# Summing a group's gathered tiles in the opposite order, and two Ifs in a row for two paths

## The chip, the cores and the metric

The kernel runs on one core of one Trainium2 chip. The metric is the device time of one execution in microseconds (us), the median of several executions; lower is better. The profile comes from one further execution under the hardware profiler, which has a time of its own.

## The reference

One layer of a graph network on N = 12500 nodes with D = 256 features and E = 200000 edges, all in float32. The edges come sorted by destination `dst`.

```python
h = relu(layernorm(x))                       # 12500 x 256
agg = segment_sum(h[src], dst, N)            # 200000 gathered rows, summed by destination
z = (1 + eps_gin) * h + agg
t = relu(batchnorm(z @ W1 + b1, g1, bt1))    # 256 -> 512, statistics over all nodes
y = relu(batchnorm(t @ W2 + b2 + h, g2, bt2))
out = x + y
```

## The kernel before

**Two paths.** The kernel first loads `src` and `dst`, transposes them on TensorE so that each column holds the 128 edges of one tile, and tests whether the destinations are spread evenly enough. A flag of 0 or 1 comes out (L205), each engine loads it into a register (L689) and branches on it (L690). `fast()` (L263) handles even spreads, which is the case for these inputs; `general()` (L474) handles the rest and is not executed.

**Stages of `fast()`.** Nodes are handled in 25 chunks of 512 (the last has 212).

1. Layer norm: each chunk of `x` is loaded, normalized to `ht`, stored to the table `h_tab` in HBM, and transposed into `hT`, which stays in SBUF.
2. Gather stage. The 1563 edge tiles of 128 edges (the last has 64) form 131 groups of 12 (`GT`), the last of 3. `gather(i)` (L322 to L333) issues one indirect DMA per tile from POOL (L328); each fetches 128 rows of 1 KB from `h_tab` into a slice of the group's buffer `gt`. The loop over the tiles at L326 runs backwards, and the list `gs` keeps the tiles in that order of issue. There are three such buffers (`AHEAD + 1`), so the gathers of group i can start only when the sums of group i - 3 have read theirs.
3. `sums(i)` (L349 to L372): VectorE makes the one-hot matrices `oh` of the group (L353); then one float32 matmul per tile adds its rows into the 128 x 256 PSUM tile `ps` (L361 to L365), in the order of `gs`. The trace records each float32 matmul as two weight loads and two matmuls, so a group has 24 records of L362. ScalarE copies `ps` to `zs` (L367), and VectorE makes the placing matrix `at` (L369).
4. `put(i)` (L374 to L389): two matmuls (four records, L380) spread the group's sums over a window of 280 nodes in `pz`, and VectorE adds the window to the chunks' `zc` (L389).
5. `first_layer(c)` (L391 to L404): once a chunk is complete, eight matmuls (16 records, L397) make `t = z @ W1`; VectorE takes statistics (L401), ScalarE copies (L402), and SP stores to `t_tab` in HBM (L403).
6. Second layer (L428 to L446) after the first batch norm's statistics are complete, and the output stage (L454 to L472) after the second's.

**What sets the order of the work.** The loop at L409 to L420 writes it out: the gathers of group i + 2, the sums of group i, the placing of group i - 1, then any chunk that is complete. A tile scheduler merges it into one queue per engine, each of which runs in order. In the queue of TensorE the first one or two tiles of a group's sums can stand ahead of a chunk's `first_layer`. POOL's queue holds, in this stage, only gathers.

**Semaphores.** A DMA adds to one of eight semaphores of the gathers in turn, so the semaphore of a gather is also that of the gather eight earlier, and POOL waits for that one before it reuses it. In the built program each matmul of L362 waits for the semaphore of its own tile's gather and then adds 1 to TensorE's own count. The two branches issue different numbers of DMAs; so that all counts agree where the branches meet, the program of before adds the difference at the start of the fast branch, for the gathers by eight instructions on POOL, one ahead of each of the first eight gathers.

Of the kernel before, what the change touches and what calls it, by code (L numbers as in the profile page):

```python
# [28 lines left out]
def kernel(  # L29
# [27 lines left out]
    for g in range(NCH):  # L57
        rows = min(CH, N - g * CH)
# [204 lines left out]
    def fast():  # L263
        with ExitStack() as fs:
# [32 lines left out]
            with ExitStack() as es:  # L297
# [51 lines left out]
                def sums(i):  # L349

                    t0, n = groups[i]
                    oh = sel.tile([P, GT, P], F32, name="oh")
                    nc.vector.tensor_tensor(  # L353
                        oh[:, :n, :],
                        col[:, :P].unsqueeze(1).to_broadcast([P, n, P]),
                        dstT[:, t0 : t0 + n].unsqueeze(2).to_broadcast([P, n, P]),
                        op=OP.is_equal,
                    )
                    ga, gs = gathered.pop(i)
                    ps = ps_s.tile([P, D], F32, name="ps")  # L360
                    for k, (j, rows) in enumerate(gs):  # L361
                        nc.tensor.matmul(  # L362
                            ps, lhsT=oh[:rows, j, :], rhs=ga[:rows, j, :], start=(k == 0),
                            stop=(k == n - 1),
                        )  # L365
                    zs = sel.tile([P, D], F32, name="zs", bufs=3)
                    nc.scalar.copy(zs, ps)  # L367
                    at = sel.tile([P, WIDE], F32, name="at")
                    nc.vector.tensor_scalar(  # L369
                        at, col, shift[:, i : i + 1], None, op0=OP.is_equal  # L370
                    )
                    summed[i] = zs, at  # L372
# [36 lines left out]
                for i in range(NG + 1):  # L409
                    if i + AHEAD < NG:  # L410
                        gather(i + AHEAD)
                    if i < NG:
                        sums(i)
                    if i == 0:
                        continue
                    put(i - 1)
                    nxt = span(i)[0] if i < NG else N
                    while done < NCH and min((done + 1) * CH, N) <= nxt:
                        first_layer(done)
                        done += 1  # L420
# [266 lines left out]
                    move(nc.scalar, ot, out, g, store=True)  # L687

    off = nc.values_load(flag, min_val=0, max_val=1, skip_runtime_bounds_check_because="it is 0 or 1")  # L689
    with tc.If(off == 0) as cmp:  # L690
        fast()
    with cmp.Else():
        general()


# [28 lines left out]
```

## Time and profile before

| | us |
|---|---|
| median of 3 runs (2385.66 to 2388.86) | 2385.85 |
| the profiled execution, its own time | 2652.91 |
| its span, first to last instruction | 2651.0 |
| first gather starts | 149.12 |
| last gather starts | 2361.34 |
| first matmul of the second layer starts | 2392.04 |

| engine | busy us | share of the span |
|---|---|---|
| PE (matmul) | 1623.6 | 61% |
| POOL | 1483.4 | 56% |
| PEld (weight load) | 1029.4 | 39% |
| DVE | 633.8 | 24% |
| ACT | 346.8 | 13% |

The gather stage, from 149 to about 2363 us, is over four fifths of the span. How to read the views: a group of instructions has its busy time and the mean of one in ns, then the idle time of its engine just before it and what ended most of that. "issue" means that nothing which the profile shows ended the wait; "remote", in the chain "another core or an unknown queue", that the releaser could not be told. PEclk and the clock column of the stretches are the granted TensorE clock as a share of full speed. [...] A row of the timeline has start us, duration us, engine, line, operation, out<-in, count, and in brackets the idle time before it with its releaser. The ends of matmuls are modelled; their starts are recorded.

### The profile page before, as it was taken

The page shows a single profiled execution, that of the slowest core. Times are in us where ns is not written, and L with a number is a line of the kernel's source. Part 1 is how long each engine was busy: PE and PEld are TensorE (multiplying, and loading weights), DVE is VectorE, ACT ScalarE, POOL GpSimd, SP SyncE. Part 2 cuts the span into 40 slices and gives each one's busy share as a digit, 9 for nine tenths or more (in the row PEclk, how much of TensorE's full clock was granted, in tenths as well). Part 3 has the DMA queues.
Part 4 walks back from the last instruction along what each step waited for, and adds up shares of the span by engine and source line. Part 5 has one row for each costly group of instructions (what it writes and reads, how often), then busy time and mean ns, then how long its engine had stood idle before and what let it go on. Part 6 is the DMA issues. An engine that isn't in the chain of part 4 may idle for free.

```text
span 2651.0 us, 14241 instructions
## 1 busy us (share of the span) xinstructions
PE 1623.6 (61%) x4881; PEld 1029.4 (39%) x4881; DVE 633.8 (24%) x1017; ACT 346.8 (13%) x561; POOL 1483.4 (56%) x1575
## 2 busy tenths in 40 slices
PE   3564556755665576556456556666565656569985
PEld 2333344433443343334334334434343334444444
DVE  6611121211221122112112112121121212124443
ACT  4710000000000000000000000000000000004446
POOL 0056667666766666666676676666666676640000
PEclk6566677776776786767777766767776677779985
DMA  5633333333333333333333333333333333325437
GB/s 176 227 101 90 95 101 115 105 95 101 115 105 95 111 105 105 96 111 105 107 97 109 106 98 102 110 105 112 95 105 110 91 114 102 111 78 214 159 130 281
DMA packets 101342, 310.96 MB, mean 117 GB/s; under 512 B 27684, under 2 KB 32362, under 8 KB 95118
## 3 DMA queue, kind: packets, MB, share of 16 engines
q0 software_dynamic: 75008, 204.90, 26.3%
q1 hardware_dynamic: 21744, 91.21, 9.6%
q10 hardware_dynamic: 4510, 13.86, 1.3%
q8 instruction: 41, 0.67, 0.1%
q14 instruction: 39, 0.32, 0.0%
HBM read 258.66 MB, written 51.20 MB: 117 GB/s over the span
## 4 chain that ended last, share of the span: by engine, by line
issue 28%; PE 26%; POOL 25%; another core or an unknown queue 9%; DMA 3%; DVE 2%; ACT 2%; ACTq 0%; POOLq 0%
POOL gt L328 25%; PE ps L362 13%; PE py L441 6%; PE ph L397 4%; DMA gt<-h_tab,srcT 3%; PE pz L380 2%; ACT yr L460 2%; DVE oh L353 1%; PE po L467 1%; DVE zc L389 1%; DVE ot L471 0%; DVE mv L229 0%; DVE at L369 0%; DVE st L401 0%
## 5 line engine op out<-in xcount | busy, mean ns | idle before, releaser
L328 POOL DMA_INDIRECT gt<-h_tab,srcT x1563 | 1481.8, 948 | 850.5 <-issue 458.2
L362 PE MATMUL ps<-gt,oh 128*128 128x256 f32 x3126 | 987.1, 447 | 643.0 <-issue 559.4
L362 PEld LDWEIGHTS ps<-gt,oh 128*128 128x128 f32 x3126 | 672.5, 221 | 949.5 <-issue 738.8
L389 DVE TENSOR_TENSOR zc<-pz,zc 128x560 f32<-128x560 f32 (+9 forms) x203 | 101.0, 527 | 1518.0 <-PE ps L362 863.5
L380 PE MATMUL pz<-at,zs 128*128 128x280 f32 x524 | 194.5, 498 | 181.4 <-DVE zc L389 114.8
L367 ACT COPY zs<-ps 128x256 f32<-128x256 f32 x131 | 48.9, 373 | 1739.4 <-PE ps L362 1147.3
L397 PE MATMUL ph<-zc,w1s 128*128 128x512 f32 (+1 forms) x400 | 197.0, 648 | 80.4 <-DVE zc L389 56.9
L353 DVE TENSOR_TENSOR oh<-col,dstT 128x1536 f32<-128x1536 f32 x131 | 227.8, 1739 | 14.5 <-issue 14.5
L380 PEld LDWEIGHTS pz<-at,zs 128*128 128x128 f32 x524 | 119.5, 237 | 235.0 <-issue 209.2
L441 PE MATMUL py<-tT,w2s 128*128 128x512 f32 (+1 forms) x400 | 169.5, 587 | 4.6 <-ACT tT L434 4.6
L397 PEld LDWEIGHTS ph<-zc,w1s 128*128 128x128 f32 x400 | 82.4, 211 | 181.1 <-issue 117.5
L401 DVE BATCH_NORM_STATS2 st<-ph 128x6 f32<-128x512 f32 (+1 forms) x100 | 68.4, 684 | 265.9 <-remote 93.7
L441 PEld LDWEIGHTS py<-tT,w2s 128*128 128x128 f32 x400 | 76.4, 192 | 97.7 <-issue 86.7
L402 ACT COPY ts<-ph 128x512 f32<-128x512 f32 (+1 forms) x100 | 57.3, 573 | 334.0 <-DVE st L401 251.9
L285 PE MATMUL pz<-ident,ht 128*128 128x128 f32 (+1 forms) x200 | 65.0, 442 | 54.1 <-ACT ht L259 19.5
L434 ACT ACTIVATE tT<-ti,of,sc 128x512 f32<-128x512 f32 (+1 forms) x100 | 72.3, 796 | 91.3 <-issue 86.4
L467 PE MATMUL po<-ident,yr 128*128 128x128 f32 (+1 forms) x200 | 47.6, 413 | 35.6 <-ACT yr L460 35.6
L285 PEld LDWEIGHTS pz<-ident,ht 128*128 128x128 f32 (+1 forms) x200 | 36.6, 205 | 82.5 <-ACT ht L259 40.7
L369 DVE TENSOR_SCALAR at<-col,shift 128x280 f32<-128x280 f32 x131 | 65.5, 500 | 0.0
L460 ACT ACTIVATE yr<-hT,of,sc 128x512 f32<-128x512 f32 (+1 forms) x50 | 59.9, 1276 | 20.1 <-DVE ot L471 19.2
L445 DVE TENSOR_TENSOR hT<-py,hT 128x512 f32<-128x512 f32 (+1 forms) x50 | 33.9, 678 | 100.9 <-PE py L441 100.9
L467 PEld LDWEIGHTS po<-ident,yr 128*128 128x128 f32 (+1 forms) x200 | 37.5, 214 | 45.7 <-ACT yr L460 45.7
(68 smaller groups left out, 307.6 us busy)
## 6 DMA issues: line engine op xcount, KB each, us to landing
gt<-h_tab,srcT POOLq DMA_INDIRECT x1563
t_tab<-ts SPq DMA_DIRECT2D x24, 1024.0 KB
ti<-t_tab SPq DMA_DIRECT2D x24, 1024.0 KB
xt<-in_x_dram SPq DMA_DIRECT2D x24, 512.0 KB
h_tab<-ht SPq DMA_DIRECT2D x24, 512.0 KB
xr<-in_x_dram SPq DMA_DIRECT2D x24, 512.0 KB
out_dram<-ot ACTq DMA_DIRECT2D x24, 512.0 KB
rawi_d<-in_dst_dram SPq DMA_DIRECT2D x1, 768.0 KB
```

The costliest lines, as they stand in the source:

```text
L285: nc.tensor.transpose(pz[:, d, c * w : (c + 1) * w], ht[:w, c, d * P : (d + 1) * P], ident[:w, :w],)
L328: nc.gpsimd.indirect_dma_start(out=ga[:rows, t - t0, :], out_offset=None, in_=h_tab, in_offset=bass.IndirectOffsetOnAxis(ap=srcT[:rows, t ...
L353: nc.vector.tensor_tensor(oh[:, :n, :], col[:, :P].unsqueeze(1).to_broadcast([P, n, P]), dstT[:, t0 : t0 + n].unsqueeze(2).to_broadcast([P ...
L362: nc.tensor.matmul(ps, lhsT=oh[:rows, j, :], rhs=ga[:rows, j, :], start=(k == 0), stop=(k == n - 1),)
L380: nc.tensor.matmul(pz[:, d, :WIDE], lhsT=zs[:, d * P : (d + 1) * P], rhs=at, start=True, stop=True)
L389: nc.vector.tensor_add(side, pz[:, :, a - lo : b - lo], side)
L397: nc.tensor.matmul(ph[:, :n], lhsT=w1s[:, d, f * P : (f + 1) * P], rhs=zc[c][:, d, :n], start=(d == 0), stop=(d == DC - 1),)
L401: nc.vector.bn_stats(st1[:, f, c, :], ph[:, :n])
L434: nc.scalar.activation(tT[:, f, :n], ti[:, f, :n], AF.Relu, bias=of1[:, f : f + 1], scale=sc1[:, f : f + 1],)
L441: nc.tensor.matmul(py[:, :n], lhsT=w2s[:, f, d * P : (d + 1) * P], rhs=tT[:, f, :n], start=(f == 0), stop=(f == HC - 1),)
L460: nc.scalar.activation(yr[:, d, :, :w], hT[g][:, d, :].rearrange("p (w c) -> p c w", c=R), AF.Relu, bias=of2[:, d : d + 1], scale=sc2[:, d ...
L467: nc.tensor.transpose(po[:w, c, d * P : (d + 1) * P], yr[:, d, c, :w], ident)
```

## The change

There are two edits. The matmuls of a group go through the list of gathers from its end: the first matmul of a group uses the tile that was gathered last. Loop order and instruction count are otherwise the same, and so is the order of the lines in TensorE's queue. The path is chosen by two Ifs, one after the other, each without an Else.

```diff
@@ def sums(i)
                     ga, gs = gathered.pop(i)
                     ps = ps_s.tile([P, D], F32, name="ps")
-                    for k, (j, rows) in enumerate(gs):
+                    for k, (j, rows) in enumerate(reversed(gs)):
                         nc.tensor.matmul(
                             ps, lhsT=oh[:rows, j, :], rhs=ga[:rows, j, :], start=(k == 0),
                             stop=(k == n - 1),
@@ end of tile_gnn_kernel
     off = nc.values_load(flag, min_val=0, max_val=1, skip_runtime_bounds_check_because="it is 0 or 1")
-    with tc.If(off == 0) as cmp:
+    with tc.If(off == 0):
         fast()
-    with cmp.Else():
+    with tc.If(off == 1):
         general()
```

In the program that is built from it, the order of a group's waits changes as follows: in a full group the first matmul waits for the gather that was issued last; the next seven wait for semaphores of earlier gathers, the last four carry no wait, and only the last matmul of the group adds to TensorE's count. The eight semaphore-adding instructions ahead of the first gathers are gone from POOL. At the end of the fast path every engine branches to the second If, compares, and jumps over the general path into a short block that makes up its counts: one addition each on POOL, ACT, PE and DVE, eight on SP, and one instruction on POOL for the gathers' semaphores; then the program ends as before.

## Prediction

> **What bounds the kernel now.** I read the chain of waits first, then the group of gathers, then who makes POOL wait.
>
> ```profile
> issue 28%; PE 26%; POOL 25%; another core or an unknown queue 9%; DMA 3%; DVE 2%; ACT 2%; ACTq 0%; POOLq 0%
> ...
> L328 POOL DMA_INDIRECT gt<-h_tab,srcT x1563 | 1481.8, 948 | 850.5 <-issue 458.2
> ```
>
> The chain alternates between POOL and PE: in the profiled execution each sometimes waits for the other. The waits of POOL, with columns total us, times, longest:
>
> ```profile
> POOL gt L328 <- issue: 458.2, 1501, 0.6
> POOL gt L328 <- PE ps L362: 194.0, 42, 9.6
> ...
> POOL gt L328 <- remote: 78.7, 17, 6.6
> ```
>
> The first row is the regular gap of 0.30 us between gathers. A gather thus costs 0.95 + 0.30 = 1.253 us start to start (149.12 to 2361.34 holds 1562 steps, less the long waits), a group of twelve 15.04 us. The other two rows are 59 waits for a buffer that the sums have not released: 272.7 us, of which 59 x 0.30 = 17.7 is the regular gap, so 255.0 us are excess.
>
> Two timelines show how PE gets late. First PE in step with the gathers, then, hundreds of us later, a slow stretch and its end:
>
> ```profile
> 149.12 1.10 POOL L328 DMA_INDIRECT gt<-h_tab,srcT  x1 [119.06 <-DVE col L310]
> 152.43 2.15 PE L362 MATMUL ps<-gt,oh 128*128 128x256 f32 x4 [5.26 <-DVE oh L353]
> ...
> 185.90 0.70 PE L362 MATMUL ps<-gt,oh 128*128 128x256 f32 x2 [0.66 <-DMA gt<-h_tab,srcT]
> ...
> 187.15 0.70 PE L362 MATMUL ps<-gt,oh 128*128 128x256 f32 x2 [0.55 <-DMA gt<-h_tab,srcT]
> ```
>
> ```profile
> 1009.91 0.58 PE L362 MATMUL ps<-gt,oh 128*128 128x256 f32 x1 [2.21 <-issue]
> ...
> 1012.71 0.58 PE L362 MATMUL ps<-gt,oh 128*128 128x256 f32 x1 [2.22 <-issue]
> ...
> 1017.26 0.94 POOL L328 DMA_INDIRECT gt<-h_tab,srcT  x1 [6.11 <-PE ps L362]
> ...
> 1054.03 6.98 PE L362 MATMUL ps<-gt,oh 128*128 128x256 f32 x24
> ```
>
> A tile can be multiplied 3.3 us after its gather starts (152.43 - 149.12). In step, PE makes one pair of records per 1.25 us and its idle time ends with the DMA. In the slow stretch a record comes every 2.8 us and the wait is "issue": the tiles are there, PE just doesn't go on. POOL ends up waiting 6.11 us. A group with all its tiles landed takes 6.98 us for its 24 records in one burst, at a clock that rises from 0.50 to 0.85 as it runs.
>
> The profiled execution took 2652.9 us, the median is 2385.85, 267 less. Without the excess waits of POOL it would be 2652.9 - 255.0 = 2397.9, and 2390 without the slow matmuls at the stage's end (worked out below). That is within 0.2% of the median. So I read the timed runs as having almost no waits of POOL: there the stage is 1563 gathers at POOL's own pace, and the slow stretches belong to the profiled execution. This is an inference from one sum.
>
> **What the Trainium skill says.** "TensorE: Matmul & The Clock Gate", Part 1: TensorE runs at half clock until it has been busy for about 3.4 us. The trace agrees in kind: 0.50 while PE waits tile by tile, up to 1.00 in bursts. But half clock doubles a spacing of 0.224 us to 0.45, so it doesn't explain 2.8 us. "Perfetto Trace Analysis", section on SWDGE DMA instructions: the record ends when the descriptors are made, not when the data land; hence the 3.3 us against a record of 0.95. "Runtime: NRT & Kernel Launch", Instruction fetch mechanics: a taken branch outside the two pages held costs a fetch; no row shows its price. "Advanced Engine Details and Errata", Control Flow Timing: a branch is about 51 ns, compare and branch about 108 ns.
>
> **The change, part by part.**
>
> *Waits in the sums.* Before, a matmul of L362 waited for its own tile; now the first waits for the group's last gather and the rest run through. No matmul is added or removed. Queued behind that wait on PE are the placing of the group before (L380) and, once per 5.2 groups, a chunk's first layer (L397). For these wait VectorE's additions (L389), ScalarE's copies, SP's store, and POOL for the buffer. POOL comes last: group i + 3 reuses the buffer 1.25 + 2 x 15.04 = 31.3 us after the last gather of group i starts. The sums now end 3.3 + 7.0 = 10.3 us after it, 21 us early; with a first layer ahead of them (7.0 warm, 14.1 if half clock doubles it) still 7 us early or more. So POOL gains no wait.
>
> *Does PE keep up?* Per group 7.0 for the sums, 1.1 to 2.2 for L380 and 25/131 of 7.0 to 14.1 for the first layer: 9.5 to 11.9 us of 15.04. Were PE at half clock throughout, the sums would be 24 x 0.45 = 10.8 and the total 15.7, that is 0.7 us over, or 86 us in 131 groups; but the burst above shows the clock rising within a group. I cost this step at nothing; POOL's pace hides it.
>
> *The end of the stage*, where POOL hides nothing. Rows of before (slow as they are):
>
> ```profile
> 2361.34 0.95 POOL L328 DMA_INDIRECT gt<-h_tab,srcT  x1 [0.30 <-issue]
> ...
> 2373.51 7.03 PE L397 MATMUL ph<-zc,w1s 128*128 128x512 f32 x16
> ...
> 2392.04 8.25 PE L441 MATMUL py<-tT,w2s 128*128 128x512 f32 x15 [4.62 <-ACT tT L434]
> ```
>
> The last full group's last gather starts at 2357.62 and lands at 2360.9. PE in step is done with it at 2361.8, with two tiles of the last group at 2364.1, with the first layer of chunk 23 after 7.0 (warm) to 10.5 us (half of it at half clock), so 2371.1 to 2374.6. From its end to the second layer the trace has 2392.04 - 2380.54 = 11.5 us: 2382.6 to 2386.1 (the middle, 2384.4, is 7.6 before 2392.04; hence the 2390 above). Now the burst starts at 2360.9: sums until 2367.9, L380 1.1, two tiles 0.9, first layer 7.0 since PE is warm, 2376.9; plus 11.5 is 2388.4. So the end moves by 2.3 to 5.8 us. I take 3.0, as PE in step is usually at half clock. Its bounds: -2 if the old end is wholly cold, +10 if the new one is.
>
> *Two Ifs.* The eight instructions gone from POOL stood inside the 119.06 us in which it waits for `h_tab` before the first gather: nothing, either way. At the end SP gets a branch, a compare and eight additions to semaphores after the last store has landed. The rows nearest are the first If:
>
> ```profile
> 28.41 0.14 DVE L205 TENSOR_SCALAR flag<-some 1x1 int32<-1x1 f32 x1
> ...
> 29.30 1.79 DVE L108 TENSOR_TENSOR dstT<-dstT,base 128x1572 f32<-128x1572 f32 x1 [0.75 <-DVE flag L205]
> ```
>
> 0.75 us with loading the flag. Lower bound 0.16 (the skill's 51 and 108 ns), as an addition of work can't gain here; upper 3 us, if a page must be fetched at about the 3.3 us of a gather. I take 0.8.
>
> Sum: +3.0 + 0.8 = +3.8 us. Against the median, whose reading as a run without waits stands above: 2385.85 + 3.8 = 2389.7 us. In the profiled execution's own terms it is 2390 + 3.8 = 2394 if POOL doesn't wait, and up to 2657 if the slow stretches come back.
>
> **The rivals.**
>
> *The waits are in the timed runs too.* Then a gather must cost less there, and ending the tile by tile waits would free all 255 us: 2389.7 - 255.0 = 2134.7 us. For: the profile shows these waits, and PE in step precedes each slow stretch. Against: the time less the waits matches the median by chance only. Chance 0.14.
>
> *A few are left.* If three waits of POOL, each 255.0/59 = 4.3 us, occur in a timed run and go, 2389.7 - 13.0 = 2376.7. For: PE in step is always near being late. Against: three runs within 3.2 us of each other. Chance 0.09.
>
> *Slower: the last burst is cold.* One mechanism, at the end of the stage: PE has idled some 5 us before the last full group, so the sums run at half clock, 10.8 for 6.98 (+3.8), and half the first layer (+3.5): 2389.7 + 7.3 = 2397.0. It decides once the stage's end moves by more than 4 us. For: gather stage clock 0.72 on average. Against: 6.98 was itself a burst from half clock. Chance 0.20.
>
> **How the numbers follow.** The forecast has 0.57, with its own range 2385 to 2394. About 0.2% (4.8 us) is what a measurement of this kernel can tell from no change. Of the forecast's 0.57, 0.01 is faster, 0.37 within, 0.19 slower; the first rival gives 0.14 faster; the second 0.08 faster and 0.01 within; the third 0.19 slower and 0.01 within. Sums: 0.23, 0.39, 0.38. The range runs from 2375 (second rival) to 2400 (third, with the dear branch); the first rival is left out, with 0.03 for PE at half clock throughout.
>
> **What would show it.** Right: in the new profile matmuls of L362 run in bursts of 24 that start some 3.3 us after a group's last gather starts; waits for the DMA once per group; POOL's gathers still 1.25 us apart; the second layer starts about 27 us (2388.4 - 2361.34) after the last gather starts. The step on the end is wrong if that distance falls to 24 us or less. The reading of the median is wrong if the time falls by over 1%: then PE did hold POOL in timed runs. The step "PE keeps up" is wrong if POOL waits for PE and the time rises by tens of us.

## The result and the profile after

The changed kernel takes 2391.11 us (median of 18 runs, 2389.86 to 2393.26); the kernel before took 2385.88 beside it (18 runs). The ratio is 1.0020, 95% interval [1.0013, 1.0028]: about 5 us slower. A second measurement gave 2391.36 against 2386.42, ratio 1.0021 [1.0012, 1.0029].

The chips that the runs fell on are of two kinds: on some the kernel before takes 2386 to 2387 us, on others 2655 to 2667. Judged by its time and its waits, the profile of before (2652.91 us) is of the second kind, and the profile of after is of the first. So the two profiles can't be subtracted; each run below is compared with the kernel before on its own chip.

The profiled execution of the changed kernel took 2390.96 us (span 2389.1). Its chain of waits, then the groups of the gathers and of the sums:

```profile
POOL 58%; issue 24%; PE 8%; ACT 2%; DVE 1%; DMA 0%; ACTq 0%; POOLq 0%
...
L328 POOL DMA_INDIRECT gt<-h_tab,srcT x1563 | 1477.6, 945 | 594.7 <-issue 475.7
L362 PE MATMUL ps<-gt,oh 128*128 128x256 f32 x3126 | 914.3, 460 | 737.0 <-DMA gt<-h_tab,srcT 735.4
```

The chain is POOL's almost alone: 58% in gathers, 24% in the gaps between them. PE's idle time ends with the DMA. In the profile of before it ended with "issue":

```profile
L362 PE MATMUL ps<-gt,oh 128*128 128x256 f32 x3126 | 987.1, 447 | 643.0 <-issue 559.4
```

That difference is the chip's and not the edit's: experiment 1 has a profile of the old order on the first kind of chip, and there too the idle time ends with the DMA. Who makes POOL wait (total us, times, longest):

```profile
POOL gt L328 <- issue: 475.7, 1562, 0.3
POOL gt L328 <- DVE col L310: 119.0, 1, 119.0
```

1562 gaps of 0.30 us and the one wait before the first gather; no wait for a buffer. The timeline shows the new pattern:

```profile
164.37 0.94 POOL L328 DMA_INDIRECT gt<-h_tab,srcT  x1 [0.30 <-issue]
...
167.32 7.30 PE L362 MATMUL ps<-gt,oh 128*128 128x256 f32 x24 [18.79 <-DMA gt<-h_tab,srcT]
```

The first line is the last gather of the first group. Its data are there 2.95 us later, and the group's 24 records run in one burst of 7.30 us. The end of the stage:

```profile
2102.04 7.62 PE L362 MATMUL ps<-gt,oh 128*128 128x256 f32 x24 [5.78 <-DMA gt<-h_tab,srcT]
2102.86 0.95 POOL L328 DMA_INDIRECT gt<-h_tab,srcT  x1 [0.30 <-issue]
...
2109.50 1.11 PE L380 MATMUL pz<-at,zs 128*128 128x280 f32 x4
2110.44 1.03 PE L362 MATMUL ps<-gt,oh 128*128 128x256 f32 x4
2111.30 7.03 PE L397 MATMUL ph<-zc,w1s 128*128 128x512 f32 x16
...
2130.22 10.12 PE L441 MATMUL py<-tT,w2s 128*128 128x512 f32 x19 [4.61 <-ACT tT L434]
```

From the last gather's start to the second layer's first matmul it is 2130.22 - 2102.86 = 27.36 us. On this kind of chip POOL's pace is 1.250 us a gather in all kernels with three buffers, so this distance is what tells them apart, and it is used below.

### The profile page after: what moved, and what is told of

Same layout as the page of the kernel before. It is cut to its first block, busy times and chain, and to the rows that moved or that the text cites. A ratio compares the mean times of both kernels' runs of the same rounds, so it can differ in the third digit from the quotient of the medians.

```text
span 2389.1 us, 14246 instructions
## 1 busy us (share of the span) xinstructions
PE 1526.9 (64%) x4881; PEld 1072.4 (45%) x4881; DVE 634.9 (27%) x1017; ACT 346.3 (14%) x561; POOL 1479.3 (62%) x1575
## 4 chain that ended last, share of the span: by engine, by line
POOL 58%; issue 24%; PE 8%; ACT 2%; DVE 1%; DMA 0%; ACTq 0%; POOLq 0%
POOL gt L328 58%; PE py L441 7%; ACT yr L460 2%; PE po L467 1%; DVE ot L471 0%; PE ps L362 0%; PE ph L397 0%; DVE mv L229 0%; PE pz L380 0%; ACTq L87 0%; DMA gt<-h_tab,srcT 0%; DMA h_tab<-ht 0%; ACT ht L259 0%; DVE st L446 0%; DVE hT L445 0%
## 5 line engine op out<-in xcount | busy, mean ns | idle before, releaser
L362 PE MATMUL ps<-gt,oh 128*128 128x256 f32 x3126 | 914.3, 460 | 737.0 <-DMA gt<-h_tab,srcT 735.4
L362 PEld LDWEIGHTS ps<-gt,oh 128*128 128x128 f32 x3126 | 724.1, 236 | 931.2 <-issue 768.5
L397 PE MATMUL ph<-zc,w1s 128*128 128x512 f32 (+1 forms) x400 | 209.4, 684 | 0.5 <-DVE zc L389 0.5
L380 PE MATMUL pz<-at,zs 128*128 128x280 f32 x524 | 145.1, 399 | 0.7 <-DVE zc L389 0.7
L397 PEld LDWEIGHTS ph<-zc,w1s 128*128 128x128 f32 x400 | 93.2, 234 | 109.0 <-issue 103.9
L380 PEld LDWEIGHTS pz<-at,zs 128*128 128x128 f32 x524 | 99.4, 190 | 20.2 <-ACT ts L402 1.2
L460 ACT ACTIVATE yr<-hT,of,sc 128x512 f32<-128x512 f32 (+1 forms) x50 | 59.8, 1274 | 19.1 <-DVE ot L471 18.2
```

The source lines that it names most:

```text
L362: nc.tensor.matmul(ps, lhsT=oh[:rows, j, :], rhs=ga[:rows, j, :], start=(k == 0), stop=(k == n - 1),)
L380: nc.tensor.matmul(pz[:, d, :WIDE], lhsT=zs[:, d * P : (d + 1) * P], rhs=at, start=True, stop=True)
L397: nc.tensor.matmul(ph[:, :n], lhsT=w1s[:, d, f * P : (f + 1) * P], rhs=zc[c][:, d, :n], start=(d == 0), stop=(d == DC - 1),)
L460: nc.scalar.activation(yr[:, d, :, :w], hT[g][:, d, :].rearrange("p (w c) -> p c w", c=R), AF.Relu, bias=of2[:, d : d + 1], scale=sc2[:, d ...
```

## The experiments

My theory: the time is POOL's 1563 gathers plus an end; the opposite order costs only at the end, by the burst of the last full group (group 129), and the second If costs next to nothing. Rivals: the waits of POOL are in the timed runs too; the loss is the second If; the loss is spread over the stage.

**1. Each edit alone.** First the order alone, the If with its Else kept:

```diff
-                    for k, (j, rows) in enumerate(gs):
+                    for k, (j, rows) in enumerate(reversed(gs)):
```

> The order of the sums is reversed, the paths stay If and Else. Mine (the end of the stage +3.0 us by the order, the second If +0.8 us): about 3 to 4.5 us over before, second layer starting some 27 us after the last gather starts, no wait of POOL in the profile, profiled time about that of the timed runs. Rival 'it is all the second If': 0 to 1 us over before. Rival 'it is all the order': 5 us over before.

Measured: 2391.98 against 2387.34, ratio 1.0019 [1.0012, 1.0027]. Then the two Ifs alone, in the order of the gathers:

```diff
-    with tc.If(off == 0) as cmp:
+    with tc.If(off == 0):
         fast()
-    with cmp.Else():
+    with tc.If(off == 1):
         general()
```

> Two Ifs in a row, the order of the sums stays that of the gathers. Mine: 0.8 us over before, at most 3. Rival 'all the second If': 5 us over before. Rival 'all the order': 0. In the profile PE is in step with the gathers: if waiting tile by tile is what makes the profiled execution slow, it is again near 2650 us with POOL waiting for PE some 250 us; if that came from the additions at the start of the fast branch, or from chance, it is near 2388 us.

Measured: 2387.8 against the same 2387.34, ratio 1.0001 [0.9993, 1.0009]. So the loss is the order's; what the second If costs can't be told from nothing. This run also gives a profile of the old order on the first kind of chip. The end of its timeline:

```profile
2098.24 0.70 PE L362 MATMUL ps<-gt,oh 128*128 128x256 f32 x2 [0.56 <-DMA gt<-h_tab,srcT]
...
2100.69 3.77 PE L362 MATMUL ps<-gt,oh 128*128 128x256 f32 x6 [0.28 <-DMA gt<-h_tab,srcT]
...
2104.13 0.95 POOL L328 DMA_INDIRECT gt<-h_tab,srcT  x1 [0.30 <-issue]
2104.25 2.07 PE L380 MATMUL pz<-at,zs 128*128 128x280 f32 x4
...
2107.59 7.03 PE L397 MATMUL ph<-zc,w1s 128*128 128x512 f32 x16
...
2126.11 14.46 PE L441 MATMUL py<-tT,w2s 128*128 128x512 f32 x28 [4.61 <-ACT tT L434]
```

PE is in step to the end. The distance is 2126.11 - 2104.13 = 21.98 us, 5.38 less than in the changed kernel. (The kernel of experiment 3, also in the old order, has 1962.72 - 1941.35 = 21.37.) In the run with the order alone it is 2129.04 - 2102.40 = 26.64, 4.66 more than here. The measured medians differ by 5.2 and 4.6 us. And the old order, tile by tile, makes POOL wait for nothing here: its wait view has 51 entries for PE, 15.5 us in all, longest 0.3, which is the regular gap put down to PE.

From the page of the same run, the matmuls of the sums and the granted clock of TensorE (each digit is a fortieth of the span, in tenths of full speed):

```profile
L362 PE MATMUL ps<-gt,oh 128*128 128x256 f32 x3126 | 1215.6, 501 | 407.4 <-DMA gt<-h_tab,srcT 389.4
PEclk7557778877878888777887878788778788889986
```

In the old order PE waits for the DMA 664 times, at most 2.5 us each, and in the new order 128 times, at most 18.8 us each. The clock in the gather stage has a mean of 0.80 in the old order and of 0.78 in the new one.

**2. The last full group in the old order**, all others in the new one, the Else kept:

```diff
-                    for k, (j, rows) in enumerate(gs):
+                    for k, (j, rows) in enumerate(gs if i == NG - 2 else reversed(gs)):
```

> As order only, but the last full group (129 of 0 to 130) is summed in the order of its gathers. Mine: the cost is the burst of that one group, so the time is that of before within 1.5 us, and the second layer starts 21 to 25 us after the last gather starts. Rival 'the cost is spread over the stage' (POOL's pace, or a wait in many groups): 3 to 5 us over before, as with the order alone.

Measured: 2388.55 against 2387.34, ratio 1.0005 [0.9997, 1.0013]: by the medians most of the loss is gone with one group of 131, 1.2 us are left of 4.6. The rest of its end:

```profile
2103.52 0.95 POOL L328 DMA_INDIRECT gt<-h_tab,srcT  x1 [0.30 <-issue]
...
2106.39 1.27 PE L362 MATMUL ps<-gt,oh 128*128 128x256 f32 x4 [2.17 <-DMA gt<-h_tab,srcT]
2107.46 8.60 PE L397 MATMUL ph<-zc,w1s 128*128 128x512 f32 x16
```

The last group, still in the new order, waits 2.17 us for its last gather ahead of the first layer, and the first layer takes 8.60 where it took 7.03. The distance is 2127.95 - 2103.52 = 24.43 us: by this measure 2.45 of the 4.66 us are still there, more than the median's 1.2 and within its interval (up to 3.1). So the loss lies in the last two groups. Where group 129 no longer bursts, the last group's own new order, which the burst had hidden, costs a part of it.

**3. One tile fewer per full group.** The kernel before, without the gather and the matmul of the last tile of each of the 130 full groups; those edges are missing from the sums.

```diff
-                    for t in reversed(range(t0, t0 + n)):
+                    for t in reversed(range(t0, t0 + n - (n == GT))):
...
-                            stop=(k == n - 1),
+                            stop=(k == len(gs) - 1),
```

> The kernel before, with the last tile of each of the 130 full groups left out: its gather and its matmul are not done, so those edges are missing from the sums. Mine (timed runs are bound by POOL's pace, 1.253 us a gather): 130 x 1.253 = 162.9 us less, about 2223 us, 0.932 of before. Rival 'PE holds POOL in the timed runs as in the profile, and a gather costs less there': PE's slow stretch goes tile by tile, so the fall is at least a tenth apart from that, most likely 1/12 of the stage as a whole or 184 us with the waits, 2202 us or less.

Measured: 2224.1 against 2387.34, ratio 0.9318 [0.9304, 0.9332], that is 163.2 us less, where 130 x 1.253 is 162.9. The timed runs go at POOL's pace, 163.2 / 130 = 1.255 us a gather, and the sum leaves no room for further waits.

**4. What the spare time of the buffers hides.** The changed kernel with two buffers for gathered groups where it has three, on the first kind of chip:

```diff
-AHEAD = 2
+AHEAD = 1
```

> The changed kernel with two buffers for three, for the case that before takes 2387 us on this chip. Theory (the opposite order costs nothing in the stage only because POOL's buffer wait has 21 us to spare): 16 of 24 first layers stand behind the first tile of a group, whose sums then end 16.9 us after the last gather starts, against 16.3 at which POOL is due: 0.6 to 1.5 us each, 10 to 25 us in all, 2401 to 2416 us. Rival: 2391, no wait of POOL for PE. If before takes 2667 us here: 2665 again, both.

Measured: 2409.0 against 2386.42, ratio 1.0093 [1.0077, 1.0110]; the changed kernel with its three buffers took 2391.36 beside it, so 17.6 us come from the third buffer's absence. Who makes POOL wait:

```profile
POOL gt L328 <- issue: 466.9, 1533, 0.3
...
POOL gt L328 <- PE ps L362: 21.9, 15, 1.9
```

15 waits where 16 were expected, 21.9 - 15 x 0.30 = 17.4 us of excess. One of them in the timeline:

```profile
362.57 1.19 PE L362 MATMUL ps<-gt,oh 128*128 128x256 f32 x2 [6.01 <-DMA gt<-h_tab,srcT]
363.55 8.51 PE L397 MATMUL ph<-zc,w1s 128*128 128x512 f32 x16
371.90 4.91 PE L362 MATMUL ps<-gt,oh 128*128 128x256 f32 x22
...
377.09 0.94 POOL L328 DMA_INDIRECT gt<-h_tab,srcT  x1 [1.42 <-PE ps L362]
```

The group's first tile waits for its last gather, a first layer of 8.51 us stands between it and the other eleven, and the sums end at 376.81; POOL goes on at 377.09. Three buffers hide just this. Whether the old order would lose as much with two buffers was not tried on this kind of chip. Its trace (second run of experiment 1) has the sums of every full group done at most 6.3 us after the group's last gather starts, and two buffers make POOL wait only past 16.3 us; from that I estimate no loss. The run of the changed kernel beside it:

> The changed kernel, unchanged, for the case that this chip is like the one on which the kernel before takes 2667 us. There the trace of the changed kernel with two buffers shows TensorE's updates at the end of every second group reaching ScalarE, VectorE and POOL 9 to 10 us after the last matmul's recorded end; with two buffers POOL is due 16.3 us after a group's last gather starts and so waits 4.4 us at every second group. Theory (the stall is lateness of updates against the buffer's due time): with three buffers POOL is due 31.3 us after it, later than 10.4 + 10 = 20.4, or 29 behind a first layer; so the changed kernel does not wait, and takes 2391 to 2400 us where before takes 2667. Rival (the chip's DMA or POOL is slow as such, whatever the order): it takes 2650 us or more, with the waits in another place. If before takes 2387 us here, both expect 2391.

Its chip was of the first kind: 2391.36, no wait for a buffer, a burst of 8.05 us in group 129 and a distance of 27.85 us.

**5. What makes the profile of before slow.** These runs fell on the second kind of chip. The kernel before once more:

> The kernel before, unchanged, profiled once more. Theory: the slow stretches of TensorE, and with them 255 us of waits of POOL, belonged to one profiled execution; the span is now 2385 to 2390 us, as with the two Ifs and the old order (2386.7), and POOL waits for nothing but its own issue. Rival: the branches of one If together with waiting tile by tile make every profiled execution slow; the span is again above 2600 us and POOL again waits for PE some 50 times.

Measured: 2665.61 us with the profile, and 2667.07 in the timed runs (39) on the same chip. The theory falls: it isn't the profiled execution alone, since every timed run on this chip is as slow. (Each chip was used at one time only, so "chip" may also stand for a condition of that time.) The rival, that one If with waiting tile by tile makes the profiled execution slow, falls by experiment 3: that kernel has both, and its profiled execution took 2223.66 us, its timed runs 2224.1. Who makes POOL wait here:

```profile
POOL gt L328 <- issue: 456.6, 1496, 0.6
POOL gt L328 <- PE ps L362: 214.4, 46, 8.0
...
POOL gt L328 <- remote: 63.2, 16, 6.7
```

Then three kernels on the same chip: group 129 alone in the new order, and the changed kernel and the kernel before with two buffers.

```diff
-                    for k, (j, rows) in enumerate(gs):
+                    for k, (j, rows) in enumerate(reversed(gs) if i == NG - 2 else gs):
```

> The kernel before with one group of 131 summed in the opposite order: the last full one. Theory (the loss lies at the end of the stage, in this group's burst alone): the whole loss of the order is there, +4 to +5 us against before, near 2391, and in the profile the second layer starts some 27 us after the last gather starts, where it was 22.0 with every group in the order of its gathers. Since PE has been waiting tile by tile until then, its clock may be lower and the burst up to 1 us longer. Rival (the loss is spread over the groups, or comes with a different first layer): within 2 us of before, and a distance of 22 to 24 us.

> The changed kernel with two buffers for gathered groups where it has three, so that the slack of POOL's buffer wait shrinks from 31.3 to 16.3 us after a group's last gather starts. In the profile of the changed kernel a group with a first layer ahead of most of its sums ends them 16.9 us after its last gather starts, one without 10.4 us. Theory (the opposite order costs nothing in the stage only because POOL's wait for the buffer has 21 us to spare): with two buffers, the 16 of 24 chunks whose first layer stands behind the first tile of a group make POOL wait for PE, 0.6 to 1.5 us each, so 10 to 25 us in all and some 2401 to 2416 us. Rival (the sums never come near POOL, the slack does not matter): no more than the three-buffer kernel, 2391, with no wait of POOL for PE.

> The kernel before with two buffers where it has three, in the order of the gathers. Theory: PE in step ends a group's sums some 4 us after its last gather starts, and even behind a first layer of 7 to 8 us it has caught up by 13 us, before the 16.3 us at which POOL wants the buffer; no wait of POOL, within 0.1% of before, near 2386. Rival (waiting tile by tile leaves PE near being late, as the slow profile of before suggested): POOL waits for PE here too, and the time rises by 10 us or more.

Measured against 2667.07: 2667.24 (ratio 0.9997 [0.9989, 1.0005]), 2664.94 (0.9989 [0.9982, 0.9995]) and 2659.74 (0.9966 [0.9949, 0.9983]). All three stay slow. For their own questions these runs say little, since some 260 us of waits lie over them. But the changed kernel with two buffers shows where POOL's waits come from:

```profile
1006.54 8.07 PE L362 MATMUL ps<-gt,oh 128*128 128x256 f32 x24 [10.83 <-DMA gt<-h_tab,srcT]
...
1021.49 2.05 PE L362 MATMUL ps<-gt,oh 128*128 128x256 f32 x4 [5.94 <-DMA gt<-h_tab,srcT]
1023.79 0.37 ACT L367 COPY zs<-ps 128x256 f32<-128x256 f32 x1 [28.56 <-remote]
...
1023.98 0.95 POOL L328 DMA_INDIRECT gt<-h_tab,srcT  x1 [4.40 <-remote]
```

The burst ends at 1014.61 by the records, yet ScalarE's copy of its result starts at 1023.79, 9.2 us later, and POOL goes on only then. In the changed kernel on the first kind of chip that copy starts 0.1 us after the burst. Here it starts more than 1 us after it in 72 of the 131 groups, and POOL waits 72 times, in all but one case until 0.2 us after such a copy starts. From this I made a theory, that TensorE's updates come late and that a third buffer would cover it, and tried it with the changed kernel, only group 129 half in each order:

```diff
-                    for k, (j, rows) in enumerate(reversed(gs)):
+                    for k, (j, rows) in enumerate(gs[:6] + gs[:5:-1] if i == NG - 2 else gs[::-1]):
```

> The changed kernel, in which the last full group alone goes half in each order: its first six tiles in the order of their gathers, its last six from the end. If before takes 2387 us on this chip: theory (the loss is the part of the last full group's sums that is left when its last gather lands): after that landing half a burst is left, some 3.5 to 4 us instead of 7.6, so about half the loss, +2 to +3 us against before, near 2389, and the second layer starts 24.5 to 25.5 us after the last gather. Rival (the last group's order does not matter): +4.6 to +5 as for the changed kernel. If before takes 2667 us here: this is the changed kernel but for a few us, and the theory of late updates expects 2390 to 2400 with no wait of POOL for a buffer, while the rival (the chip's gathers are slow as such) expects 2650 or more.

Measured, on another chip of the second kind: 2648.6 against 2654.58, ratio 0.9966 [0.9952, 0.9979]. The theory falls: a third buffer does not cover the lateness. Who makes POOL wait:

```profile
POOL gt L328 <- issue: 460.0, 1507, 0.6
POOL gt L328 <- remote: 221.3, 47, 7.6
...
POOL gt L328 <- PE ps L362: 47.0, 8, 6.2
```

Again 55 waits, 268.3 us. Neither the order nor the number of buffers moves that sum much. At its end, which was undisturbed, the split group did about what was expected: 12 records, 4.54 us (3.5 to 4 expected), after the landing, and a distance of 2385.82 - 2360.38 = 25.44 us (24.5 to 25.5 expected). The last run, beside it, was group 129 alone in the new order again:

> The kernel before with only the last full group summed in the opposite order, for the case that before takes 2387 us on this chip. Theory: the whole loss of the order comes from this one group, +4 to +5 us against before (a colder clock may add up to 1 us), and the second layer starts some 27 us after the last gather starts. Rival (the loss is spread over the groups): within 2 us of before, a distance of 22 to 24 us. If before takes 2667 us here: 2667 again, both.

2652.22 against 2654.58, ratio 0.9988 [0.9978, 0.9998]. Its last burst takes 8.35 us and its distance is 2391.91 - 2363.79 = 28.12 us, of the changed kernel's size. The old order has only one end on these chips to set beside it, that of the kernel before with two buffers, 2398.03 - 2376.48 = 21.55 us; it fits, but POOL had waited 6.43 us two gathers before its last one. So it is experiment 2 that places the loss in the last two groups; that group 129 alone can make all of it rests on this one distance, from a chip of the second kind.

## Why the prediction was right, and what in it was not

The time (2389.7 forecast, 2391.11 measured) came out by its mechanism: POOL's pace hides the new order in the stage, and the end moves. The size of the move was not as good: +3.8 us forecast, +5.2 measured. By its steps:

**The reading of the median** as a run without waits was right for the chips that were timed: a tile fewer per group saves 163.2 us where 162.9 were worked out, and the new profile has no wait for a buffer. The reason given for the slow profile was wrong: "the slow stretches belong to the profiled execution". On chips of the second kind the timed runs are as slow as the profiled ones. The forecast survived because the median, not the profile, was the base of the sum, and because the profile's rows at the end of the stage, from the first layer on, are the same on both kinds of chip (7.03 us, then 11.5 to the second layer in the old order). That was luck as much as method.

**Waits in the sums, PE keeps up.** Right: bursts, 128 waits of PE for the DMA, no wait of POOL. The sums end 10.6 us after the group's last gather starts (the median; 10.3 forecast) and at most 18.2, behind a first layer, so 13 of the 31.3 us are to spare. The burst starts 2.9 us after that gather and not 3.3: the prediction took 3.3 from a row whose wait ended with `oh`, not with the gather. That the spare time is what hides the new order is shown by experiment 4: without the third buffer the changed kernel takes 17.6 us more. The half clock after idling, which the Trainium skill states ("TensorE: Matmul & The Clock Gate", Part 1), shows in this trace: a burst takes 8.43 us after 6.67 us idle, 5.42 after 1.47, and the 22 records that follow a first layer take 4.91. (The prediction's burst at 1054.03, read as ending at 0.85 of the clock, has 1.00 from 1058 on.) In the stage no burst is slow enough to hold up POOL. At the end it is a part of the loss: at 5.42 us, group 129's burst of 7.62 would have ended 2.2 us earlier, an estimate.

**The end of the stage** was right in kind and too small: +3.0 taken, 4.7 to 5.4 measured between the distances. The new end was forecast well. Its first layer was to start 2369.9 - 2361.34 = 8.6 us after the last gather; it started 8.44 after it in the changed kernel, 7.72 with the order alone. The old end was the mis-sized term. Taking +3.0 for a new end at 2388.4 - 2361.34 = 27.06 us means an old one at 24.06, and it was at 21.98. Its row was "the first layer of chunk 23 after 7.0 (warm) to 10.5 us (half of it at half clock)". That layer started 2107.59 - 2104.13 = 3.46 us after the last gather (2364.1 - 2361.34 = 2.76 in the prediction) and took 7.03, although PE had been working tile by tile. So the upper part of "2.3 to 5.8" was the true one. The choice of 3.0 rested on "PE in step is usually at half clock", and that was wrong. In step on the first kind of chip the granted clock has a mean of 0.80, and even the profile of before, from 185 to 190 us, where the prediction shows PE in step, has 1.00. At the end the clock was 0.50 from 2100 to 2104, but with the last tiles, L380 and the last group's tiles PE was busy from 2100.69 on, 6.9 us before the first layer, and during that layer it was 1.00. The bound "+10 if the new one is" wholly cold doesn't follow from the prediction's own terms either: 3.0 + 3.8 for the sums + 7.1 for the first layer + 2.0 for L380 and the two tiles is 15.9. Nothing near it was measured.

**Two Ifs**: 0.8 taken; the measured ratio 1.0001 [0.9993, 1.0009] allows -1.7 to +2.1 us. It isn't refuted, and not confirmed as more than zero.

**The rivals.** "The waits are in the timed runs too" fell for the chips timed; on the other kind they are there, but the new order does not free them (0.9966 for a kernel that has it in all groups but half of one), which the rival also needed. "The last burst is cold" has a small part: 7.62 and 8.05 us were measured for the burst where 6.98 was taken, 6.88 with the order alone. Its half-cold first layer did not occur in the new order (7.03 in all three).

**What stays open**: why TensorE works in slow stretches on some chips. In the old order the gathers' records (948 ns there, 946 on the other kind), the time of the DMA engines that the gathers' packets take (26.6% of 2663.8 us, 29.6% of 2386.7) and the second layer (171.0 us busy, 170.1) are as on the other chips. The late updates were seen, not explained.

## What to carry to other kernels

If one engine's pace hides a stage, ask for an edit's cost where the stage ends and nothing hides it any more: here the last two groups of 131 carried the loss. Consuming in the opposite order of arrival turns twelve short waits into one long one; here that was free in the stage, where the third buffer left time to spare, and made the end a burst later. Before subtracting two profiles, compare each profile's own time with the median; if they differ by more than a few per cent, take the old form's profile again, or build on the median.

## What was not expected of the hardware

The same program took 2387.34 us on one chip and 2667.07 on another (12% more), in 36 and 39 runs that each agree within 1%. On the slow ones POOL waits 52 to 72 times for buffers, 268 to 292 us in all, with both orders and with two or three buffers. Either the records of single matmuls are 2.8 us apart, or a whole burst runs in time and its completion reaches ScalarE, VectorE and POOL together late: in the changed kernel with two buffers by more than 1 us in 72 of 131 groups, in 56 of them by 8.8 to 10.6. In 55 of these 56 the copy starts about 2 us (1.9 to 2.5) after the next group's first matmul starts; what connects the two is open. On such a chip the sign of the small effect may be another: the kernel nearest to the changed one was 0.3% faster there than before. But so was the kernel before with two buffers, in the old order, so it isn't shown that the order is the cause. The changed kernel itself was not run on one.
